# First attention layer of a recommendation kernel as one product per sample, with a four-stage pipeline in source order

## The chip, the cores and the metric

The kernel runs on one core of one Trainium2 chip. The metric is the device time of one execution in microseconds (us). A profile is one execution taken by the hardware profiler; "granted clock" is the share of full TensorE speed that the profile records. Engines in the profile: PE is TensorE, PEld its weight loads, DVE VectorE, ACT ScalarE, POOL GpSimd, SP SyncE.

## The reference

Cut to what matters. B is 16384 samples, F = 69 tokens a sample, E = 96; the first layer has 64 outputs.

```python
u = emb[batch_user]                          # (B, 69, 96), gathered rows
ql = emb[batch_label[:, 0]]                  # (B, 96)
q = broadcast(ql)
z = concatenate([q, u, q - u, q * u])        # 384 wide
h = dice(z @ W1 + b1, a1)                    # first attention layer, 64 wide
att = (h @ W2 + b2) @ W3 + b3
pre = where(batch_user < ITEM_NUM, u * att, 0)
pooled = einsum("gf,bfe->bge", window, pre)  # 10 groups
...                                          # top network: 1056 -> 200 -> 80 -> 1
```

With W1 in four blocks of rows Wq, Wu, Wd, Wp, the first layer before dice is u (Wu - Wd) + (q * u) Wp + q (Wq + Wd) + b1. Below, A is Wu - Wd and Cq is Wq + Wd.

## The kernel before

It works on blocks of 128 samples: 69 tiles of 128 tokens in 18 chunks of up to four tiles, two chunks making a pair, so nine pairs a block. Each tile is fetched by one indirect DMA on GpSimd (a "gather" of 128 rows of 96 floats), transposed by PE, and goes through the hidden layer, the attention weight and the pooling.

```python
def pair_part1(bi, pr, ids, qT):
    u = upool.tile([P, 8, E], F32, tag="u", name=f"u{name}")       # 10 buffers
    ph = ps_h.tile([P, 512], F32, tag="h", name=f"ph{name}")
    for j in range(2):                        # the two chunks: two column halves of PE
        ...
        for i, t in enumerate(ch):
            gather(u[:, 4 * j + i, :], ids[:, bi * NT + t : bi * NT + t + 1])
            nc.tensor.transpose(ptr[:, i * P : (i + 1) * P], u[:, 4 * j + i, :], ident)
        nc.scalar.copy(uT[k][0:E, :], ptr[:, 0:n])
        times_q(quT, uT[k][0:E, :], ch[0] * P, n, qT)      # VectorE: u * q, per sample
        o = ph[j * H1 : (j + 1) * H1, 0:n]
        nc.tensor.matmul(o, caug[bi % 2][:, k, :], uT[k], start=True, stop=False)
        nc.tensor.matmul(o, Wp, quT[:, 0:n], start=False, stop=True)
    ...                                       # dice on ScalarE and VectorE -> y
# pair_part2: attention weights from y (PE), times the masks (VectorE), pooling (PE)
# main loop: part 1 of a pair, then part 2 of the pair before; order left to the framework
```

## Time and profile before

| | before |
|---|---|
| time, median of 3 | 16139.71 us |
| PE busy | 77% |
| POOL busy | 53% |
| VectorE, ScalarE busy | 24%, 19% |
| mean granted clock | 0.598 |
| chain of waits, by engine | PE 60%, unknown release 29% |

The chain is followed back from the last instruction, at each step to what released it; "another core or an unknown queue" in it is a wait whose release the profile doesn't find. The rows of groups read: line, engine, operation, tiles, count, busy us, mean ns of one, then the idle time ahead of them and what ended most of it. The prediction below shows the lines.

Two of its terms, as the trace of the kernel before shows them. "Half clock": the view by windows has a granted clock of 0.50 from 5050 to 5084 us, and 1.00 from 5000 to 5014. "The lock": a gather that starts while VectorE is idle takes 0.946 us in the median; of 466 that start inside L268 (both inputs in SBUF) 255 take over 0.98 us, the longest 1.44; of 347 inside L316 (one input in PSUM) none does.

### The profile page before, as it was taken

Reading aid. Unit: us, or ns where it says so; the run is one execution under the profiler, and the core shown is the slowest. Engines: PE = TensorE matmul, PEld = TensorE weight load, DVE = VectorE, ACT = ScalarE, POOL = GpSimd, SP = SyncE. Lnnn points to the kernel's source line nnn. Section 1 sums busy time; section 2 is a strip of 40 time slices with the busy share of each in tenths; the row PEclk is TensorE's granted clock in tenths of the full one; section 3 lists DMA queues with packets and bytes.
Section 4 is the critical chain, followed back from the end, with each engine's and each line's share of the span. In section 5 each row is a group of like instructions: output and inputs, shape, how many; then the busy total and the mean of one; then the engine's idle time right before and its main releaser. Section 6 shows DMA issues by size and latency. Waiting matters only on the chain.

```text
span 16189.3 us, 144750 instructions
## 1 busy us (share of the span) xinstructions
PE 12511.9 (77%) x56708; PEld 8013.8 (50%) x56708; DVE 3926.3 (24%) x12194; ACT 3123.8 (19%) x5506; POOL 8572.5 (53%) x8973
## 2 busy tenths in 40 slices
PE   6877877778777787777777777778777777787777
PEld 3554544445444554455455454545545545455445
DVE  2222222222222222222222222222222222222222
ACT  1121111111112111211111111112111111121111
POOL 5555555545555555555555555555555545555553
PEclk6566565655656565655555656565555655555656
DMA  1111111111111111111111111111111111111110
GB/s 34 29 29 27 29 29 28 29 26 28 29 28 28 28 29 28 29 29 28 29 28 28 28 28 29 28 29 27 29 29 28 28 27 28 29 29 27 28 29 20
DMA packets 293496, 456.76 MB, mean 28 GB/s; under 512 B 145896, under 2 KB 147151, under 8 KB 292818
## 3 DMA queue, kind: packets, MB, share of 16 engines
q0 software_dynamic: 287008, 440.98, 13.0%
q8 instruction: 453, 7.42, 0.2%
q1 hardware_dynamic: 4144, 5.15, 0.1%
q14 instruction: 225, 1.84, 0.0%
q10 hardware_dynamic: 1666, 1.37, 0.0%
HBM read 446.85 MB, written 0.07 MB: 28 GB/s over the span
## 4 chain that ended last, share of the span: by engine, by line
PE 60%; another core or an unknown queue 29%; issue 4%; DVE 3%; ACT 3%; POOL 1%; DMA 0%; SPq 0%; DVEq 0%; ACTq 0%; POOLq 0%
PE acc L364 14%; PE ph L305 11%; PE ph L304 10%; PE ptr L299 10%; PE patt L327 7%; PE pc L252 3%; PE p L383 3%; ACT g L315 1%; DVE y L316 1%; ACT g L314 1%; DVE pooled L372 1%; PE p L401 1%; ACT uT L300 1%; POOL u L229 1%
## 5 line engine op out<-in xcount | busy, mean ns | idle before, releaser
L229 POOL DMA_INDIRECT u<-in_emb,ids x8832 | 8442.8, 956 | 7443.9 <-PE ptr L299 2421.4
L304 PE MATMUL ph<-uT,caug 105*64 105x512 f32 (+2 forms) x4608 | 3332.6, 894 | 2298.3 <-ACT uT L300 1640.5
L305 PE MATMUL ph<-quT,w 96*64 96x512 f32 (+2 forms) x4608 | 3264.4, 866 | 213.7 <-DVE quT L277 185.3
L364 PEld LDWEIGHTS acc<-rw,u 128*96 128x96 f32 x18176 | 2810.6, 261 | 1142.5 <-issue 522.8
L364 PE MATMUL acc<-rw,u 128*96 128x30 f32 (+2 forms) x18176 | 2853.9, 325 | 391.7 <-DVE rw L345 317.8
L299 PEld LDWEIGHTS ptr<-ident,u 128*96 128x96 f32 x8832 | 1411.3, 185 | 2518.3 <-issue 2070.5
L299 PE MATMUL ptr<-ident,u 128*96 128x128 f32 x8832 | 2290.2, 395 | 178.4 <-issue 106.9
L300 ACT COPY uT<-ptr 96x512 f32<-96x512 f32 (+2 forms) x2304 | 1279.5, 561 | 5911.8 <-PE ptr L299 3795.7
L314 ACT ACTIVATE g<-ph 128x512 f32<-128x512 f32 (+2 forms) x1280 | 719.4, 562 | 6345.9 <-remote 3263.5
L304 PEld LDWEIGHTS ph<-uT,caug 105*64 105x64 f32 x4608 | 573.2, 183 | 2632.9 <-ACT uT L300 1707.8
L327 PEld LDWEIGHTS patt<-v,y 128*128 128x128 f32 x8704 | 1660.0, 284 | 266.4 <-issue 154.5
L327 PE MATMUL patt<-v,y 128*128 128x2 f32 x8704 | 1620.8, 309 | 124.1 <-DVE y L316 116.3
L337 DVE SCALAR_TENSOR_TENSOR w<-patt,bb,mask 128x8 f32<-128x8 f32 (+2 forms) x1280 | 275.2, 223 | 5621.8 <-remote 2807.0
L268 DVE TENSOR_TENSOR quT<-uT,qT 96x414 f32<-96x414 f32 (+3 forms) x2304 | 1363.4, 592 | 2.3
L316 DVE TENSOR_TENSOR y<-ph,g 128x512 f32<-128x512 f32 (+2 forms) x1280 | 822.7, 643 | 1813.7 <-ACT g L315 1549.5
L305 PEld LDWEIGHTS ph<-quT,w 96*64 96x64 f32 x4608 | 641.6, 183 | 822.5 <-issue 444.7
L315 ACT ACTIVATE g<-g,a1c,na1c 128x512 f32<-128x512 f32 (+2 forms) x1280 | 998.9, 780 | 25.2
L277 DVE TENSOR_TENSOR quT<-uT,qT 96x29 f32<-96x29 f32 (+33 forms) x4352 | 747.1, 185 | 801.3 <-ACT uT L300 406.4
L252 PE MATMUL pc<-Cq,qT 96*9 96x64 f32 x4608 | 520.3, 305 | 378.0 <-DVE qT L246 201.5
L372 DVE COPY pooled<-acc 96x430 f32<-96x430 f32 (+1 forms) x384 | 340.0, 886 | 1672.4 <-PE acc L364 1313.9
L383 PE MATMUL p<-pooled,wf 96*100 96x128 f32 x5120 | 727.2, 307 | 22.7 <-DVE quT L277 18.3
L383 PEld LDWEIGHTS p<-pooled,wf 96*100 96x100 f32 x5120 | 700.2, 196 | 34.2 <-DVE quT L277 26.0
(53 smaller groups left out, 2737.7 us busy)
## 6 DMA issues: line engine op xcount, KB each, us to landing
u<-in_emb,ids POOLq DMA_INDIRECT x8832
ids<-in_idx SPq DMA_DIRECT2D x16, 284.0 KB
q<-in_emb,ids POOLq DMA_INDIRECT x135
wf<-in_Wf ACTq DMA_DIRECT2D x1, 825.0 KB
wt<-in_wtok ACTq DMA_DIRECT2D x1, 345.0 KB
uT<-in_rows SPq DMA_DIRECT2D x16, 18.0 KB
out<-res SPq DMA_DIRECT2D x16, 4.0 KB
ts<-in_tsamp ACTq DMA_DIRECT2D x1, 103.5 KB
```

The source lines that it names most:

```text
L229: nc.gpsimd.indirect_dma_start(out=dst, out_offset=None, in_=emb, in_offset=bass.IndirectOffsetOnAxis(ap=index, axis=0),)
L252: nc.tensor.matmul(pc[E : E + NS, k, :], qT[:, s0 : s0 + NS], Cq, start=True, stop=True)
L268: nc.vector.tensor_tensor(dst[:, at : at + m * F].rearrange("e (m f) -> e m f", f=F), src[:, at : at + m * F].rearrange("e (m f) -> e m f" ...
L299: nc.tensor.transpose(ptr[:, i * P : (i + 1) * P], u[:, 4 * j + i, :], ident)
L300: nc.scalar.copy(uT[k][0:E, :], ptr[:, 0:n])
L304: nc.tensor.matmul(o, caug[bi % 2][:, k, :], uT[k], start=True, stop=False)
L305: nc.tensor.matmul(o, Wp, quT[:, 0:n], start=False, stop=True)
L315: nc.scalar.activation(gs, gs, AF.Identity, bias=a1c[lo:hi], scale=na1c[lo:hi])
L316: nc.vector.tensor_mul(y[lo:hi, 0:n], ph[lo:hi, 0:n], gs)
L327: nc.tensor.matmul(patt[:, :, i], y[:, cols], v2, start=True, stop=True)
L364: nc.tensor.matmul(acc[gi][:, (x - a) * G : (z - a) * G], u[:, 4 * j + i, :], rw[:, j, i, (x - lo) * G : (z - lo) * G], start=False, stop= ...
L383: nc.tensor.matmul(p1[:, i, :], wf1[:, k, i * DH : (i + 1) * DH], pooled[:, k, :] if k < G else qT, start=(k == 0), stop=(k == G),)
```

## The change

The intent is to relieve PE. For each sample s a matrix M_s = A + diag(q_s) Wp, with a 97th row q_s Cq + b1, is built by VectorE one block ahead. The hidden layer is then one product per sample instead of two products over all columns of a chunk, and the pieces of the two column halves alternate so that they can run side by side, as two products of different halves do in the trace before (L304 and L305 at 5052.84 us, 1.11 us each). Four stages (fetch, hidden, attend, pool) are one pair apart, and every engine issues in source order.

```diff
-            quT = cpool.tile([E, 512], F32, tag="quT", name=f"quT{name}_{j}")
-            times_q(quT, uT[k][0:E, :], ch[0] * P, n, qT)
-            o = ph[j * H1 : (j + 1) * H1, 0:n]
-            nc.tensor.matmul(o, caug[bi % 2][:, k, :], uT[k], start=True, stop=False)
-            nc.tensor.matmul(o, Wp, quT[:, 0:n], start=False, stop=True)
...
+    def build(qT, M, a, b):
+
+        m = M[0:E, a:b, :]
+        nc.vector.tensor_tensor(
+            m,
+            Wp.to_broadcast([E, b - a, H1]),
+            qT[:, a:b].rearrange("e (m o) -> e m o", o=1).to_broadcast([E, b - a, H1]),
+            ALU.mult,
+        )
+        nc.vector.tensor_tensor(m, m, A.to_broadcast([E, b - a, H1]), ALU.add)
...
+        both = [pieces(2 * pr), pieces(2 * pr + 1)]
+        for n in range(max(map(len, both))):
+            for j in range(2):
+                if n < len(both[j]):
+                    s, a, b = both[j][n]
+                    nc.tensor.matmul(
+                        ph[j * H1 : (j + 1) * H1, a:b],
+                        M[:, s, :],
+                        uT[:, j * 512 + a : j * 512 + b],
+                        start=True,
+                        stop=True,
+                    )
...
+    with tc.manual_schedule():
...
+        for i in range(total + 6):
+            if at := part(i, 3):
...
+                pool(i - 3, pr, us.pop(i - 3), rws.pop(i - 3), accs[n])
+            if at := part(i, 2):
...
+                rws[i - 2] = attend(i - 2, n % NB, pr, round_of(n)[1], ys.pop(i - 2))
+            if at := part(i, 1):
...
+                ys[i - 1] = hidden(i - 1, pr, Ms[n])
...
+            if at := part(i, 0):
+                n, pr = at
+                us[i] = fetch(i, n % NB, pr, round_of(n)[0])
...
+                    if pr in BUILD:
+                        build(qTs[n + 1], Ms[n + 1], *BUILD[pr])
```

The builds come in five bursts a block (pairs 4 to 8) of a multiply and an add over 26 or 25 samples. The 97th row goes through DRAM by SyncE.

## The prediction

> **What bounds the kernel now.** I read the page first (busy shares, chain, groups), then the timeline of some stretches, the rows by form, the waits, and last distances between starts counted over the whole trace. A block is 128 samples; there are 128 blocks, so the span of 16189 us is 126.5 us a block. From the page:
>
> ```profile
> PE 12511.9 (77%) x56708; PEld 8013.8 (50%) x56708; DVE 3926.3 (24%) x12194; ACT 3123.8 (19%) x5506; POOL 8572.5 (53%) x8973
> ...
> PEclk6566565655656565655555656565555655555656
> ...
> PE 60%; another core or an unknown queue 29%; issue 4%; DVE 3%; ACT 3%; POOL 1%; DMA 0%; SPq 0%; DVEq 0%; ACTq 0%; POOLq 0%
> ...
> L229 POOL DMA_INDIRECT u<-in_emb,ids x8832 | 8442.8, 956 | 7443.9 <-PE ptr L299 2421.4
> L304 PE MATMUL ph<-uT,caug 105*64 105x512 f32 (+2 forms) x4608 | 3332.6, 894 | 2298.3 <-ACT uT L300 1640.5
> L305 PE MATMUL ph<-quT,w 96*64 96x512 f32 (+2 forms) x4608 | 3264.4, 866 | 213.7 <-DVE quT L277 185.3
> ```
>
> TensorE carries 60% of the chain at a mean clock of 0.6. Its two largest matmuls, the hidden layer of L304 and L305, are each recorded twice for an f32 product: 2 x 4608 records of 0.87 to 0.89 us. The gathers (L229) sit idle 7444 us, mostly waiting for PE to free `u` (L299, L364). So **PE bounds it, and POOL is the next bound**. The 29% are waits whose release the profile doesn't find. In the row of waits for ACT at L314 they come to 3263 us:
>
> ```profile
> ACT g L314 <- remote: 3263.5, 202, 31.5
> ```
>
> They are late PE semaphores: in the timeline below PE's last hidden matmul before the stall ends near 5057 and the activation that waits for it starts at 5079.
>
> ```profile
> 5050.32 0.63 DVE L268 TENSOR_TENSOR quT<-uT,qT 96x483 f32<-96x483 f32 x1
> ...
> 5050.37 1.40 POOL L229 DMA_INDIRECT u<-in_emb,ids  x1 [0.30 <-issue]
> ...
> 5052.84 1.11 PE L305 MATMUL ph<-quT,w 96*64 96x512 f32 x1
> ...
> 5052.84 1.11 PE L304 MATMUL ph<-uT,caug 105*64 105x512 f32 x1
> ...
> 5055.12 1.97 PE L305 MATMUL ph<-quT,w 96*64 96x512 f32 x2
> ...
> 5060.82 0.94 POOL L229 DMA_INDIRECT u<-in_emb,ids  x1 [0.30 <-issue]
> 5062.07 0.94 POOL L229 DMA_INDIRECT u<-in_emb,ids  x1 [0.30 <-DMA u<-in_emb,ids]
> ...
> 5079.15 0.60 ACT L314 ACTIVATE g<-ph 128x512 f32<-128x512 f32 x1 [25.30 <-remote]
> ```
>
> Three things are to be seen here. Gathers that wait for nothing start 1.25 us apart (0.95 busy, 0.30 issue); over the trace 7801 of 8966 distances are under 1.3 us, mean 1.2508. Two hidden matmuls of different column halves start together and run side by side. And a gather that starts just after a VectorE multiply has begun takes 1.40 us in place of 0.94.
>
> [...] of 7041 gathers that start while VectorE is idle, none takes over 0.98 us; of 347 that start inside L316 (one input in PSUM), none; of 466 inside L268 (both inputs in SBUF) 55%, and with 500 to 600 ns of the multiply still to run the median is 1.37 us. The gather gets through about 0.14 us before the multiply's recorded end. The whole loss before is 95 us. [...] 96-column loads of L364 come 0.160 us apart, 128-column ones of L327 0.213, both at the half clock.
>
> **The change part by part.** Per block:
>
> *Removed on PE*: 36 products of 512 columns or less, 72 records. At the half clock starts are 0.854 to 0.908 apart, so 61 to 65 us (less where halves overlapped); and 72 records of L252, 0.107 us each as 24 in 2.73 us show, 7.7 us:
>
> ```profile
> 4990.79 2.73 PE L252 MATMUL pc<-Cq,qT 96*9 96x64 f32 x24 [9.47 <-DVE qT L246]
> ```
>
> *Added on PE*: one product per sample and chunk. Counting the pieces of the 18 chunks gives 145, mean 60.9 columns, so 290 records, each with a 64-column load. Load: 64/96 x 0.160 = 0.107 us; stream: 61/64 x 0.107 = 0.102. Serial: 290 x 0.107 = 31 us; if the alternating halves overlap in full, 15.5 us.
>
> *Kept on PE at the half clock*: transposes 70 x 0.213 = 14.9; attention 68 x 0.213 = 14.5; pooling 142 x 0.160 = 22.7; top network about 11; the rest 1.6. **PE after: 80 to 96 us a block** at the half clock (before, by the same rule, 132 without overlap, which full-clock stretches cut). [...]
>
> *VectorE*: out go the quT multiplies (1363 + 747 us in L268 and L277, 16.5 us a block). In come ten building instructions in five bursts of a multiply and an add, 26 x 64 = 1664 columns each. From these rows the slope is (651-579)/69 = 1.04 ns a column, the fixed part 148 ns:
>
> ```profile
> L268 DVE TENSOR_TENSOR quT<-uT,qT 96x414 f32<-96x414 f32 x1152 | 667.3, 579 | 0.0
> L268 DVE TENSOR_TENSOR quT<-uT,qT 96x483 f32<-96x483 f32 x896 | 583.7, 651 | 2.3
> ```
>
> So 1.88 us each, 18.5 us a block: VectorE stays near 33 us, not a bound. But both have **both inputs in SBUF** and are three times as long as L268.
>
> *POOL*: 70 gathers a block x 1.2508 = 87.6 us, x 128 = 11207 us (8960 gathers; the 135 split label gathers become 128). This is the floor once PE is under it. To it comes the lock. In a burst the first instruction shuts a gather out until 1.74 us (1.88 - 0.14), the second from 1.80 to 3.54. A gather that wants to start at a random phase f in 0 to 1.25 starts at 1.74, its successor would at 2.99 and starts at 3.54; undisturbed that one had started at f + 1.25. Loss 3.54 - 1.25 - f, mean 1.66 us. 5 bursts x 127 blocks x 1.66 = 1055 us. The 0.4 us multiplies of L345 cost some 30 us more by the same rule.
>
> *The pipeline*: ten `u` tiles let gathers run about seven pairs ahead of the transposes, and four stages in source order give each wait between PE, ACT and VectorE about an iteration (10 us) of slack. The row through DRAM is one small write and read with iterations to spare. ACT is unchanged (24 us a block).
>
> *Sum*: first gather at 26 us + 11207 + 1055 + 30 + some 45 for the last iterations without a gather = 12363 in a profiled run; timed runs are 0.3% shorter (16140 against 16189): 12325. I add 75 us for stretches in which PE holds POOL up: **12400 us**, 23% less.
>
> **Rivals.**
> (a) *The lock costs nothing*, since gathers slip in or the builds fall into POOL's waits: 11.3 ms. For it: only 95 us are lost now. Against: that fits the short multiplies, and if POOL is the bound it has no waits to hide in.
> (b) *PE stays the bound.* For it: the late semaphores come almost only while gathers run (of waits with POOL busy in all the 8 us before, 25% are over 2 us late; with POOL idle 0.1%), and after the change gathers run all the time; pieces have 580 more PE instructions a block than the products that go, less 144 + 144. If the halves don't overlap (96 us) and late semaphores cost the chain its 29% (37 us a block) as now: 96 + 37 = 133 us, 17 ms, no gain. Against: deeper stages hide late releases, and with overlap PE has 80 us against POOL's 96. I give half of the lateness a small chance: 80 + 18 = 98 us, 12.6 ms; 96 + 18 = 114 us, 14.6 ms.
> (c) *VectorE's bursts hold PE up*: 3.7 us before the next attention step's work. They are behind the urgent multiply in source order, and an iteration has 10 us; worth perhaps 0.1 ms.
>
> **Range and chances.** The body lies between rival (a), 11.3, and a mild (b), 13.5, with the lock in the middle; I take 11500 to 13500. Faster than 2% fails only under the full (b): 0.94 faster, 0.04 same, 0.02 slower.
>
> **What would show it.** Right: POOL busy over 75% with next to no gaps for PE; gathers 1.25 us apart outside the builds, and up to 2.7 us long when they start inside one; starts of the hidden pieces in pairs a few ns apart, about 0.05 us a record; the chain on POOL. Wrong: POOL still waiting for PE's L299 or pooling (rival b), or gathers of 0.95 us inside builds (rival a). The prediction falls if PE's late semaphores grow with steady gathers, or if the halves take turns.

## More of the kernel before

The runs of this study met several chips, which the results number. This turned out to matter more than the change itself: the kernel before took 11.47 ms on three of them and 16.1 to 16.4 ms on three others.

## The result, and the profile after

| | before | after |
|---|---|---|
| median | 16130.61 us (4 runs) | 14157.77 us (4 runs) |
| lowest, highest | 16093.38, 16143.22 | 14150.18, 14178.55 |

The ratio is 0.8782, with a 95% interval of 0.8765 to 0.88: 12.2% faster. Ratios here are the mean time of one kernel's fast runs over the mean of the other's fast runs of the same rounds, so not quite the ratio of the medians. The result lies outside the predicted range, 1758 us above the predicted time. Which chip this was is not recorded; by its 16131 us before, it is of the kind called slow below.

From the page of the changed kernel: busy shares, granted clock in 40 slices, chain by engine, and the gathers.

```profile
PE 10058.7 (71%) x80260; PEld 9342.3 (66%) x80260; DVE 4441.9 (31%) x6564; ACT 3142.9 (22%) x5506; POOL 9627.4 (68%) x8966
...
PEclk8555555555555555555555555555555555555555
...
PE 41%; another core or an unknown queue 20%; POOL 17%; issue 12%; DVE 5%; ACT 3%; DMA 2%; SPq 0%; POOLq 0%; ACTq 0%; DVEq 0%
...
L222 POOL DMA_INDIRECT u<-in_emb,ids x8832 | 9480.2, 1073 | 4261.9 <-issue 2428.5
```

PE's busy time has fallen by 2.5 ms, as meant. The mean of a gather has risen from 956 to 1073 ns: 9626.7 us for all 8960, where 0.947 us each would be 8485, so about 1.14 ms of lock, which was predicted. But the gathers still sit idle for 4262 us, of which only 2429 are their own issue; the rest is waiting. The rows of waits (engine, line, what was waited for: us, times, longest) show for what:

```profile
ACT g L304 <- remote: 4204.1, 252, 50.1
...
POOL u L222 <- remote: 862.1, 259, 9.5
...
POOL u L222 <- PE acc L358: 604.5, 137, 11.6
```

"remote" is a release that the profile didn't find. The timeline of one stretch shows what it is (start, duration, engine, line, operation, tiles; at the end the idle time ahead):

```profile
5029.73 2.07 PE L288 MATMUL ph<-uT,M 97*64 97x69 f32 x32
...
5031.73 1.94 PE L274 MATMUL ptr<-ident,u 128*96 128x128 f32 x8
...
5032.74 0.95 POOL L222 DMA_INDIRECT u<-in_emb,ids  x1 [0.30 <-issue]
...
5042.75 0.94 POOL L222 DMA_INDIRECT u<-in_emb,ids  x1 [0.30 <-DMA u<-in_emb,ids]
5043.58 0.60 ACT L304 ACTIVATE g<-ph 128x512 f32<-128x512 f32 x1 [15.46 <-remote]
```

The 32 hidden records take 2.07 us, 0.065 a record where 0.05 was predicted; most start in pairs some 7 ns apart, one pair in 0.107 us, so the halves do run side by side. They end by 5031.80. The activation that waits for exactly these matmuls starts at 5043.58, about 12 us later, and nothing else holds it. Meanwhile the gathers go on 1.25 us apart.

To count this I matched each wait of ScalarE or VectorE on PE's semaphore with the matmul that brings the count, and took its start minus that matmul's recorded end. Call it **lateness**. A prompt wait has 0.04 us. After, 1169 of 2385 such waits are over 1 us late, the worst tenth over 22.9 us; before, 1337 of 4928. (The counts depend on how a wait is matched to its matmul: a second matching, tile by tile, gave 1382 of 2456 and 1141 of 4446.) One episode comes in almost every block (125 in 128), mostly at the first hidden pieces of a block, whose last matmul ends some 6 to 9 us after the last build. In the block above the gathers then run 1.25 us apart for 30 us (5025 to 5055), while the lateness grows from 12 to 25 us, until they have to wait for PE.

A matmul's end in the trace is modelled, so one may ask whether PE itself is slow or only its completion reaches the others late. The trace also records each update of PE's semaphore. In this profile 3420 of the 12142 recorded updates come within 40 ns of the one before, though no two of the matmuls that make them end within 100 ns of each other. In a profile without lateness (the changed kernel on chip 12, below) none of 13100 updates comes within 100 ns of the one before, and all but two follow a matmul's recorded end by 10 to 20 ns. The updates of ScalarE and VectorE are prompt in both profiles, 99% of them within 13 ns. (Updates that are missing from a trace, 8% here, can only widen the gaps.) So PE's completions are held back and let through in bunches, closer together than PE was ever seen to make them: at least there, it is the completion that is late. Where it is held isn't visible.

### The profile page after: what moved, and what is told of

The parts are those of the page before. It is cut to its first block, busy times and chain, and to the rows that moved or that the text cites.

```text
span 14156.7 us, 187662 instructions
## 1 busy us (share of the span) xinstructions
PE 10058.7 (71%) x80260; PEld 9342.3 (66%) x80260; DVE 4441.9 (31%) x6564; ACT 3142.9 (22%) x5506; POOL 9627.4 (68%) x8966
## 3 DMA queue, kind: packets, MB, share of 16 engines
q14 instruction: 192, 1.57, 0.0%
## 4 chain that ended last, share of the span: by engine, by line
PE 41%; another core or an unknown queue 20%; POOL 17%; issue 12%; DVE 5%; ACT 3%; DMA 2%; SPq 0%; POOLq 0%; ACTq 0%; DVEq 0%
POOL u L222 17%; PE acc L358 10%; PE ph L288 9%; PE patt L316 8%; PE ptr L274 7%; PE p L377 4%; DMA u<-in_emb,ids 1%; DVE M L263 1%; DVE M L257 1%; DVE y L306 1%; ACT g L305 1%; ACT uT L276 1%; PE p L397 1%; ACT g L304 1%
## 5 line engine op out<-in xcount | busy, mean ns | idle before, releaser
L222 POOL DMA_INDIRECT u<-in_emb,ids x8832 | 9480.2, 1073 | 4261.9 <-issue 2428.5
L316 PE MATMUL patt<-v,y 128*128 128x2 f32 x8704 | 1814.7, 327 | 2543.8 <-DVE y L306 1985.8
L288 PE MATMUL ph<-uT,M 97*64 97x69 f32 (+7 forms) x37120 | 2540.4, 304 | 897.9 <-issue 639.5
L288 PEld LDWEIGHTS ph<-uT,M 97*64 97x64 f32 x37120 | 2302.0, 213 | 1038.9 <-issue 736.5
L304 ACT ACTIVATE g<-ph 128x512 f32<-128x512 f32 (+2 forms) x1280 | 722.1, 564 | 9052.7 <-remote 4204.1
L274 PE MATMUL ptr<-ident,u 128*96 128x128 f32 x8832 | 2075.7, 399 | 220.6 <-issue 162.2
L263 DVE TENSOR_TENSOR M<-M,A 96x1664 f32<-96x1664 f32 (+1 forms) x640 | 1190.8, 1861 | 22.1
L257 DVE TENSOR_TENSOR M<-w,qT 96x1664 f32<-96x1664 f32 (+1 forms) x640 | 1184.0, 1850 | 0.0
L305 ACT ACTIVATE g<-g,a1c,na1c 128x512 f32<-128x512 f32 (+2 forms) x1280 | 999.2, 781 | 43.1
L377 PE MATMUL p<-pooled,wf 96*100 96x128 f32 x5120 | 930.9, 359 | 14.2 <-issue 12.7
L377 PEld LDWEIGHTS p<-pooled,wf 96*100 96x100 f32 x5120 | 881.9, 238 | 22.4 <-issue 17.9
L334 DVE TENSOR_TENSOR rw<-R,w 128x240 f32<-128x240 f32 (+2 forms) x1280 | 481.2, 376 | 43.8
```

Source lines behind the costliest of these rows:

```text
L222: nc.gpsimd.indirect_dma_start(out=dst, out_offset=None, in_=emb, in_offset=bass.IndirectOffsetOnAxis(ap=index, axis=0),)
L257: nc.vector.tensor_tensor(m, Wp.to_broadcast([E, b - a, H1]), qT[:, a:b].rearrange("e (m o) -> e m o", o=1).to_broadcast([E, b - a, H1]), ...
L263: nc.vector.tensor_tensor(m, m, A.to_broadcast([E, b - a, H1]), ALU.add)
L274: nc.tensor.transpose(ptr[:, k * P : (k + 1) * P], u[:, 4 * j + k, :], ident)
L288: nc.tensor.matmul(ph[j * H1 : (j + 1) * H1, a:b], M[:, s, :], uT[:, j * 512 + a : j * 512 + b], start=True, stop=True,)
L304: nc.scalar.activation(gs, ph[lo:hi, 0:n], AF.Sigmoid, scale=S_DICE)
```

## The experiments

The theories at the start: **A**, undisturbed gathers make PE's completions late; **B**, the slow stretches are PE's own, set off by its order of work, such as a new block's first products. Kernels without real gathers or builds give a wrong result. The comparison with the reference still accepted some of them, so "correct" says little about those.

### Without gathers, with plain loads, without builds, halves apart

Four edits of the changed kernel:

```diff
 e1_no_gather: ten fixed u tiles, gathered for the first ten pairs only
+                if i < 10:
                 gather(u[:, 4 * j + k, :], ids[:, ...])
 e2_plain_load: r is the first of 128 consecutive rows, another 128 for each tile
-                gather(u[:, 4 * j + k, :], ids[:, ...])
+                nc.sync.dma_start(out=u[:, 4 * j + k, :], in_=emb[r : r + P, :])
 e3_no_build:
-                        Ms[n + 1] = head_row(n + 1, qTs[n + 1])
-                    if pr in BUILD: ...
+                        Ms[n + 1] = Ms[0]
 e4_halves_apart:
-        for n in range(max(map(len, both))):
-            for j in range(2):
+        for j in range(2):
+            for n in range(len(both[j])):
```

> The changed kernel without its gathers: ten fixed u tiles, gathered once for the first ten pairs and then read again and again (wrong result on purpose, everything else kept). Theory A (the late PE semaphores come from undisturbed runs of gathers): no wait on PE is more than about 2 us late, and the kernel runs at PE's own pace, 80 to 96 us a block by my sum, so 10.3 to 12.3 ms. Theory B (the slow stretches are PE's own, set off by the first products of a new block or the like): they stay, one a block of about 22 us, so 80 + 22 = 102 us a block, about 13 ms or more.

> Each gather replaced by a plain load of 128 consecutive rows (same bytes, same u tile, issued by SyncE; wrong result on purpose). GpSimd does nothing, but the rows still arrive. Theory A1 (GpSimd's work for a gather slows PE): as without gathers, 10.3 to 12.3 ms, no late waits. Theory A2 (rows arriving in SBUF slow PE): slow stretches stay, 13 to 14.2 ms. Theory B: slow stretches stay too, 13 ms or more; the run without gathers tells A2 from B.

> The per-sample matrices and their row are made once and used for all blocks (wrong result on purpose): no builds, so no lock on the gathers. If the lock loss of 1142 us lies on the path in full: 14158 - 1142 = 13.0 ms. Theory A (undisturbed gathers make PE late): gathers run at 1.25 us everywhere, slow stretches come more often, and most of the gain is lost: 13.6 to 14.2 ms. Theory B (a new block's first products): nothing depends on the gathers, 13.0 ms, and if the first use of a freshly built matrix is what sets it off, no slow stretches and 11.4 ms.

> The hidden pieces of one column half all before those of the other, so no two neighbours run side by side. My sum has 31 us a block instead of 15.5 for the hidden pieces: if PE is on the path all the time, 15.5 us x 128 = 2.0 ms longer, 16.1 ms; if PE is on it for about half (chain PE 41% plus late semaphores 20%), 0.8 to 1.2 ms longer; if GpSimd is the bound and PE has room, 14.2 ms.

| run, chip 11 | median us | ratio to before |
|---|---|---|
| kernel before | **11475.79** | |
| no gathers | 9053.01 | 0.7889 |
| plain loads | 9454.46 | 0.8245 |
| no builds | 11288.4 | 0.9837 |
| halves apart | 12442.29 | 1.0841 |

The surprise is the first row: **the same kernel before took 11476 us here, not 16131**. In none of the four traces is a wait on PE over 1 us late. So this chip could not decide between A and B, and it asked a new question: is the lateness a matter of the chip? It did measure other terms. Without gathers PE alone sets the end; its share of the page and the chain are:

```profile
PE 8978.2 (99%) x80260; PEld 8621.2 (95%) x80260; DVE 4465.7 (49%) x6574; ACT 3108.8 (34%) x5506; POOL 214.7 (2%) x211
...
PE 98%; POOL 1%; issue 0%; DMA 0%; DVE 0%; ACT 0%; POOLq 0%
```

That is 71 us a block at a mean clock of 0.628, below the predicted 80 to 96. No builds gives 11288, beside the predicted floor of 11207 + 30 + 26 + 45 = 11308.

### The changed kernel again, builds with PSUM operands, and the framework's own order

```diff
 f2_psum_build: label and A are copied to PSUM (the small PSUM tiles share one bank)
-            qT[:, a:b].rearrange("e (m o) -> e m o", o=1)...
+            kk[:, n % 2, a:b].rearrange("e (m o) -> e m o", o=1)...
-        nc.vector.tensor_tensor(m, m, A.to_broadcast([E, b - a, H1]), ALU.add)
+        nc.vector.tensor_tensor(m, m, Ak.to_broadcast([E, b - a, H1]), ALU.add)
 f3_tile_order:
-    with tc.manual_schedule():
+    if True:
```

> The changed kernel itself, unaltered, because in the first four experiments the kernel before took 11476 us where the blind measurement had 16131, and no wait on PE was late. Theory P (late PE semaphores belong to the place the kernel runs at, not to the kernel): if the kernel before is again near 11476, this one has no late waits and is bound by GpSimd with the lock: 11288 (no builds) + about 1140 (lock) = 12.43 ms, 8% SLOWER than before; if before is near 16131, this one is at 14.16. Theory Q (the change takes PE off the bound everywhere): under 11.47 ms in either.

> The builds read the label and the constant A from PSUM, so that neither of the two instructions has both inputs in SBUF; the small PSUM tiles share one bank. Theory L (two SBUF inputs lock the gathers out): gathers stay at 0.95 us inside builds, the lock loss of about 1140 us vanishes; with no late PE semaphores 11.3 to 11.4 ms; with them between 13.0 and 14.2. Rival (any long VectorE instruction delays a gather, or the loss is elsewhere): as the changed kernel.

> The new first layer, but every engine's order left to the framework's own scheduling instead of source order. If the four-stage source order is what hides waits, PE stalls come in and this is slower than the changed kernel by 3% or more; if GpSimd with the lock is the bound anyway, it is within 1%.

| run, chip 12 | median us | ratio to before |
|---|---|---|
| kernel before | 11468.32 | |
| changed kernel | **12432.06** | 1.0841 (1.0823 to 1.0859) |
| builds with PSUM operands | **11290.35** | 0.9842 (0.9826 to 0.9859) |
| framework's own order | 12771.51 | 1.1134 |

Theory P came true: on such a chip the change makes the kernel **8.4% slower**, at 12432 us, within 0.3% of the 12400 that were predicted for the other. Chain and gathers of the changed kernel here, from its page, then a stretch with two builds from its timeline:

```profile
POOL 55%; issue 21%; DMA 13%; PE 11%; DVE 0%; POOLq 0%; ACT 0%; ACTq 0%; DVEq 0%
...
L222 POOL DMA_INDIRECT u<-in_emb,ids x8832 | 9527.9, 1079 | 2691.6 <-issue 2501.4
```

```profile
5019.14 1.87 DVE L257 TENSOR_TENSOR M<-w,qT 96x1664 f32<-96x1664 f32 x1
5019.24 2.58 POOL L222 DMA_INDIRECT u<-in_emb,ids  x1 [0.30 <-issue]
...
5021.04 1.89 DVE L263 TENSOR_TENSOR M<-M,A 96x1664 f32<-96x1664 f32 x1
5022.13 1.61 POOL L222 DMA_INDIRECT u<-in_emb,ids  x1 [0.30 <-issue]
```

POOL now has no idle time but its issue (2691.6, of which 2501 are issue), and the chain is on it. The gather at 5019.24 starts 0.10 us after the multiply, and takes 2.58 us instead of 0.95; the next runs into the add. With the PSUM operands the builds are as long, and the gathers pass straight through (1890 of them start inside a build, and none takes over 0.96 us; of 1247 in the changed kernel, all but one take over 0.98):

```profile
L232 POOL DMA_INDIRECT u<-in_emb,ids x8832 | 8386.3, 950 | 2691.5 <-issue 2469.7
```

```profile
5001.11 1.86 DVE L268 TENSOR_TENSOR M<-w,kk 96x1664 f32<-96x1664 f32 x1
...
5001.65 0.95 POOL L232 DMA_INDIRECT u<-in_emb,ids  x1 [0.30 <-issue]
...
5003.01 1.88 DVE L274 TENSOR_TENSOR M<-M,kk 96x1664 f32<-96x1664 f32 x1
```

The gathers of the two runs differ by 9648.8 - 8507.2 = 1141.6 us, and the two times by 1141.7 us. So **the lock costs 1.14 ms, is due to the two SBUF inputs, and lies wholly on the path** on this chip. The rival that any long VectorE instruction holds up a gather is refuted. Against the kernel before, the PSUM version is 1.6% faster.

The framework's own order is 2.7% slower, between the two cases I had expected. Of the 339 us, 307 are again longer gathers (9956.0 against 9648.8 us): I take it that its builds fall worse for the gathers, but didn't follow it up.

### A slow chip, first meeting

> The kernel before, unaltered, for its profile at a place where it takes about 11.47 ms. If its late semaphores are what held it at 16.1 ms, then without them GpSimd bounds it already: chain on POOL, gathers 1.25 us apart nearly everywhere, 8967 x 1.2508 = 11216 us, plus about 26 us start, 45 us drain and 95 us lock = 11.38 ms, near 11.47. If instead PE still bounds it, the chain is on PE and gathers have waits for PE of over 1 ms. If it runs where it takes 16.1 ms, its profile repeats the first one.

> The version with label and A in PSUM once more, in case this chip is one where the kernel before takes 16.1 ms. There: if late PE semaphores come from undisturbed gathers, lateness takes the lock's place and the time stays at 13.6 to 14.2 ms; if they are tied to a block's start, 14158 - 1142 = 13.0 ms. Where before takes 11.47 ms: 11.29 ms again.

> No gathers after the first ten pairs (as in the first experiment, wrong result on purpose), and the hidden pieces of one column half all before those of the other. With PE alone on the path this measures the overlap of the two halves by itself: 9053 us with halves alternating; my sum gives 15.5 us x 128 = 2.0 ms more at the half clock, less if the clock is higher (x 0.5/0.63 = 1.6 ms): 10.6 to 11.0 ms. If neighbours on different halves gain nothing, 9.05 ms. If before takes 16.1 ms here: any wait on PE over 2 us late without gathers would show that gathers are not needed for lateness.

The edit of the third is that of halves apart, on top of no gathers. Chip 8 was of the slow kind: the kernel before took 16351.84 us in the median of 7 runs (16337.85 with its profile, with 1396 of 4928 waits over 1 us late). The PSUM version, unaltered, took **14228.92** instead of 11290.35, ratio 0.8709 (0.868 to 0.8738). The lock is gone, and the time is about that of the changed kernel with the lock: lateness has taken the lock's place, as theory A had it; 2053 of 2612 waits are over 1 us late. The largest row of its waits:

```profile
ACT g L315 <- remote: 4882.5, 510, 22.4
```

Without gathers, with the halves apart, the four runs took 9069.74 to 9956.66 us, and 4 of 1958 waits were over 1 us late, all in the first 137 us, where the gathers of the first ten pairs still run. Those runs fell in different states (clocks 0.674 to 0.751), so I draw nothing from their time, except that on this slow chip, too, PE is prompt once the gathers have stopped.

### Ten kinds of work in one run

To compare everything on one chip, one kernel has stretches of 12 blocks, all with the fixed u tiles and the PSUM builds, except where named:

```diff
+    psum: gather       lock: gather, builds as in the change    none: no gather
+    load: nc.sync.dma_start of 128 rows     half: every other gather
+    slow: nc.gpsimd.memset(scr[:, 0:256], 0.0), then the gather
+    thin: gather of 8 of the 96 columns     memset: 8 x nc.gpsimd.memset(u, 0.5) a pair
+    none_apart, psum_apart: as none and psum, hidden halves one after the other
```

> One run with ten kinds of stretches of 12 blocks each (wrong result on purpose), to have all of them on one chip: (psum) gathers and builds with a PSUM operand; (lock) gathers and the change's builds; (none) no gathers; (load) plain loads by SyncE in place of the gathers; (half) every other gather; (slow) a GpSimd memset before each gather; (thin) gathers of 8 of the 96 columns; (memset) no gathers, eight GpSimd memsets of u per pair; (none_apart) and (psum_apart) as none and psum, hidden halves one after the other; last 8 blocks as psum. Where before takes 11.47 ms: psum 88 us a block, lock 97, none and load 71 to 74, half 71 to 80, none_apart 12 to 16 above none, and no late waits anywhere. Where before takes over 16 ms, theory A1 (GpSimd's work for a gather makes PE late): load without late waits, near none; thin as late as psum (about 110 us a block), half in between. Theory A2 (rows arriving in SBUF): load as late as psum, thin not late. Theory A3 (any steady GpSimd work): memset late too.

> The ten kinds of stretches again, in an order that leaves real rows in u for all but the last (psum, lock, none, load, half, none_apart, slow, psum_apart, thin, memset), because in the first such run the stretch none_apart read constants that a memset had left and had a granted clock of 0.74. If that clock came from the constants: none_apart at a clock near 0.59 and 10 us a block above none; if it came from the halves not running side by side: 0.74 again and no longer than none. Where before takes over 16 ms: theory A1 (GpSimd's work for a gather makes PE late): load near none without late waits, thin late like psum; A2 (arriving rows): load late, thin not; A3 (any steady GpSimd work): memset late too; slow tells whether gathers 1.6 us apart leave PE in time.

> The ten kinds of stretches as in the run before, for a slow place. There theory A1 (GpSimd's work for a gather makes PE late): load near none (75 us a block) without late waits, thin late like psum (about 110); A2 (arriving rows): load late, thin not; A3 (any steady GpSimd work): memset late too; slow tells whether gathers 1.6 us apart leave PE in time (102 us a block) or not (110 or more). At another place: the same as the last run, within 1 us a block.

The first two met chips 3 and 11 (before: 11476.61 and 11476.58 us), the third chip 7 (before: 16131.81). The second and third run the same kernel. Time of a block is from the starts of y's multiplies, over nine blocks of each stretch; each run is one execution, and the stretches that chips 3 and 11 share agree within 0.4 us a block, but for the two with halves apart:

| stretch | chip 11, us a block | chip 7, us a block | chip 7: waits over 1 us late |
|---|---|---|---|
| psum | 87.79 | **111.71** | 81 of 126 |
| lock | 96.49 | 114.20 | 63 of 143 |
| none | 75.09 | **74.00** | 0 of 156 |
| load | 76.21 | 75.01 | 0 of 157 |
| half | 75.11 | 79.00 | 28 of 153 |
| none_apart | 74.85 | 71.66 | 0 of 144 |
| slow | 102.11 | 106.08 | 115 of 150 |
| psum_apart | 87.48 | 113.94 | 80 of 139 |
| thin | 87.61 | 112.22 | 82 of 128 |
| memset | 75.11 | 74.22 | 0 of 154 |

On chip 11 (and chip 3) no wait is late in any stretch. On chip 7 the stretches, in the view by windows (from and to, length, then busy us and count of PE, PE loads, VectorE, ScalarE and POOL; granted clock, DMA share, GB/s): psum, none, load, thin, memset.

```profile
339.20:1344.60 1005.40, 725.88 (x5643) 678.70 (x5643) 313.59 (x470) 215.27 (x388) 598.08 (x631) 0.57 0.15 33
...
2928.40:3594.40 666.00, 657.94 (x5645) 627.77 (x5644) 315.46 (x470) 218.59 (x388) 8.52 (x9) 0.60 0.01 3
3820.80:4495.80 675.00, 661.71 (x5645) 628.72 (x5644) 315.47 (x469) 218.46 (x388) 8.52 (x9) 0.60 0.22 49
...
9279.60:10289.60 1010.00, 715.65 (x5643) 668.09 (x5643) 313.50 (x470) 215.44 (x388) 598.58 (x631) 0.58 0.07 5
10514.20:11182.20 668.00, 660.44 (x5645) 630.65 (x5644) 316.32 (x470) 218.51 (x388) 485.86 (x657) 0.60 0.02 4
```

The plain loads bring 49 GB/s, more than the gathers' 33, and PE is prompt. The thin gathers bring 5 GB/s, and PE is as late as ever. GpSimd memsets, with POOL busy 73% of the time, do nothing. A count that needs no matching agrees: of the updates of PE's semaphore, 936 of 1372 come within 100 ns of the one before in psum, 967 of 1379 in thin, 489 of 1301 in lock, and none in none, load and memset. So on the slow chips it is **the gather as such, however many bytes it brings**, that makes PE late: A1 stands; A2 (arriving rows), A3 (any GpSimd work, as far as memsets tell) and B (PE's own order) fall. Thin and load differ in the engine that issues them, GpSimd and SyncE. Which part of a gather does the harm is not shown: thin names 128 rows as psum does, and no run issued a plain DMA from GpSimd or a gather of fewer rows. The granted clock doesn't show the lateness: 0.57 and 0.60 on chip 7, 0.56 and 0.59 on chip 11.

A second finding is in none and none_apart. On chip 11, from the same view:

```profile
2392.50:3068.30 675.80, 668.32 (x5645) 637.68 (x5644) 315.79 (x470) 218.57 (x388) 8.49 (x9) 0.59 0.01 3
...
5105.30:5778.90 673.60, 666.67 (x5645) 637.74 (x5644) 312.88 (x470) 217.99 (x388) 8.81 (x10) 0.69 0.01 4
```

PE is busy 99% of both and does the same work, in 75.09 and 74.85 us a block. With the halves side by side the granted clock is 0.59, one after the other 0.69. So **running the halves side by side gains no time** here: the granted clock is lower with it. (An estimate from these numbers: 75.09 x 0.59 = 44 us of full clock against 74.85 x 0.69 = 52, so the overlap itself is real.) On chip 7 side by side was even the slower, 74.00 against 71.66 us. In the first mixed run none_apart came after a stretch that left constants in u, and had 71.65 us at 0.74; since the second run, with real rows, had 0.69, and chip 7, also with real rows, 0.74, the clock comes mainly from the order. Not from it alone: the run without gathers above had the same order on the same chip 11, and 0.628 and 71 us a block; why is open. The halves-apart kernel above, at 12442 against 12432 us on two fast chips, says nothing on this, since POOL bounds both (43% and 55% of their chains, the most of any engine).

### How much gathering PE stands

> Stretches of 12 blocks with PSUM builds: all gathers (psum), 6, 4 and 2 of each 8 (s6, s4, s2), all gathers with a GpSimd memset of 128, 256, 384, 512 columns before each (d128 to d512), eight memsets at once before each pair (pause8), and none (wrong result on purpose). Where before takes over 16 ms: if each gather costs PE a fixed time, us a block falls in a line from 112 to 74: s6 102, s4 93, s2 84, and spacing gathers out doesn't help; if only long undisturbed runs of gathers make PE late, s6 and s4 fall well below the line (the last run had 79 for 4 of 8), and d384, d512 and pause8 have no late waits and are as long as GpSimd's own work. Elsewhere: psum 88, s6 to none 75, d128 to d512 96 to 125, no late waits.

```diff
+    s6, s4, s2: 6, 4, 2 of each 8 gathers     none: no gather
+    d128 ... d512: nc.gpsimd.memset(scr[:, 0:128 ... 512], 0.0) before each gather
+    pause8: 8 memsets of 256 columns before each pair's gathers
```

Chip 10 was slow (before: 16394.71 us).

| stretch | gathers a block | us a block | waits over 1 us late |
|---|---|---|---|
| psum | 70 | 113.65 | 82 of 130 |
| s6 | 54 | 93.58 | 71 of 131 |
| s4 | 36 | 79.26 | 28 of 157 |
| s2 | 19 | 75.49 | 1 of 160 |
| none | 1 | 75.09 | 0 of 153 |
| d128 | 70 | 110.97 | 90 of 144 |
| d256 | 70 | 110.63 | 126 of 174 |
| d384 | 70 | **109.49** | **0 of 227** |
| d512 | 70 | 116.67 | 0 of 236 |
| pause8 | 70 | 115.48 | 95 of 150 |

A fixed cost per gather is refuted: s6, s4 and s2 lie at 94, 79 and 75 where a line would have 105, 95 and 85 (113.65 and 75.09 as its ends). It is the rate: at 109.49 / 70 = 1.56 us from gather to gather all waits are prompt, and POOL sets the pace; with the shorter memset, whose own pace is 1.46 us (102.11 / 70 on chip 11), 126 of 174 waits are over 1 us late. Eight gathers together and then a pause don't help, though their own pace averages about the same (an estimate: 8 x 1.25 us and eight memsets of 0.33 us, as measured on chip 3, make 1.58 us a gather). With all 70 gathers a block takes 109 to 117 us on this chip whatever is done, that is 1.56 to 1.67 us for each gather.

### The kernel before on a fast chip

> The kernel before with a profile once more; the last time it met a slow place. Where it takes 11.47 ms: GpSimd bounds it, chain mostly on POOL, gathers 1.25 us apart, no wait on PE over 1 us late; the rival is PE at a high granted clock (0.69 in the result lists, where the slow place had 0.60) with POOL waiting on it. Where it takes over 16 ms: as the first profile.

> The kernel before with a profile, for a place where it takes 11.47 ms (the last two tries met slow places). There: GpSimd bounds it, chain mostly POOL, issue and DMA as in the changed kernel's profile at 12.43 ms, gathers 1.25 us apart nearly everywhere; the rival is PE with POOL waiting on it for over 1 ms.

> The kernel before with a profile, for a place where it takes 11.47 ms. There: GpSimd bounds it, chain mostly POOL, issue and DMA, gathers 1.25 us apart nearly everywhere and 8967 x 1.2508 = 11.22 ms of them, no wait on PE over 1 us late; the rival is PE with POOL waiting on it for over 1 ms.

> The kernel before with a profile, last try for a place where it takes 11.47 ms. There: GpSimd bounds it, chain mostly POOL, issue and DMA, gathers 1.25 us apart nearly everywhere and 8967 x 1.2508 = 11.22 ms of them, no wait on PE over 1 us late; the rival is PE with POOL waiting on it for over 1 ms.

I wanted one profile of the kernel before where it takes 11.47 ms. All four met slow chips (7, 10, 10, 7), with 16192.4, 16305.73, 16297.61 and 16086.49 us and profiles like the first one. What bounds it on a fast chip is left as an estimate from the trace before: 8967 gathers x 1.2508 = 11216 us, with 26 + 45 + 95 of start, drain and lock 11.38 ms, which is 0.8% under the measured 11.47. That leaves PE next to nothing to add, by this estimate.

Medians of the kernel before, by chip (without the five extra profiled runs, 16086 to 16338 us, all on slow chips):

| chip | kernel before, us |
|---|---|
| 3, 11, 12 | 11477, 11476 and 11477, 11468 |
| 7, 8, 10 | 16132 and 16136, 16352, 16395 |
| the two measurements (chip not recorded) | 16140, 16131 |

Nothing in between was seen, and chips 7 and 11, met twice, gave the same both times.

## Why the prediction was wrong, step by step

- **The bound before, "PE bounds it, and POOL is the next bound".** True of the trace that I had, but a good part of it was lateness. On fast chips the same kernel runs at 11.47 ms, next to POOL's floor, which is 29% less. The unknown releases in the chain before were 29% too, which fits, but no run tests it. The prediction had read them rightly as late PE semaphores that come while gathers run, but not as something that another chip might not have.
- **PE after, 80 to 96 us a block.** PE alone takes 71 to 75. The term for the halves (31 us, or 15.5 if they overlap) was wrong in kind: side by side or apart, the block took 75.09 and 74.85 us, as the clock moved from 0.59 to 0.69. This didn't matter for the sum.
- **The builds, 1.88 us each.** Measured 1.85 and 1.86.
- **Two slips without effect on the sum.** The products of L252 are 36 records a block (4608 in 128 blocks), not 72, so 3.9 us and not 7.7 were removed; and 3 of the 7041 gathers with VectorE idle did take over 0.98 us.
- **POOL's floor, 11207 us plus ends.** Right: 11288 without builds and 11290 without the lock, against 11308 summed.
- **The lock, 1055 us for the builds.** Right in kind, 8% too small: 1141.6. (The 30 us for the short multiplies of L345 are in both runs of that difference.)
- **The sum, 12363, and 12400 with PE's share.** Right on a fast chip, 12432. Wrong on the chip of the result, 14158.
- **The step that failed is the last term of the sum: "I add 75 us for stretches in which PE holds POOL up".** On the slow chip this term was not 75 us but about 1.8 ms: before their starts the gathers sit idle for 4262 us there and for 2692 us on chip 12, 1.57 ms more, and PE's lateness is what they wait for. Rival (b) was right about the late semaphores, though not about halves that take turns, and its reason against was the error: "deeper stages hide late releases". They don't, because the lateness isn't a fixed delay that a stage of slack can absorb. It sets in when gathers follow each other at less than some 1.46 to 1.56 us (d256 and d384 on chip 10: 126 of 174 waits late, and 0 of 227), and, as in the block shown above, grows until the gathers have to wait. So the better the gathers are freed, the later PE gets: on chip 7, 81 of 126 waits were late in psum and 63 of 143 in lock. The prediction's own 37 us of lateness a block, added to PE alone at 74.00, makes 111, and psum on chip 7 took 111.71. That is luck: 37 us was 29% of the block before, and after the change the unknown releases are 20% of the chain, 22 us a block.
- **The sequel: the lock is almost free on a slow chip.** On chip 7, psum and lock differ by 2.5 us a block, little more than psum and psum_apart do there (2.2); on chip 11 they differ by 8.7. This is why the lock, the main term of the prediction, showed in the gathers' durations after the change but hardly set the time.
- **The direction.** "Faster" held on the slow kind of chip and is the reverse on the fast kind, where the change costs 8.4%. The prediction had a chance of 0.02 for that, since it took the base of 16.1 ms as the kernel's own.

What stays open: what in a gather holds PE's completions back on chips 7, 8 and 10 and not on 3, 11 and 12, where they are held, and whether PE itself ever stalls besides. I tried to model the lateness in the trace after the change as a backlog that each gather adds to and that drains steadily. The best fit (1.4 us a gather) had a correlation of 0.59 with the measured lateness, too little to call it shown.

The version with PSUM operands beats the kernel before on both kinds, 11290 against 11468 and 14229 against 16352. It beats the changed kernel by 9.2% on the fast kind; on the slow kind the two are close (111.71 against 114.20 us a block within one run, and 14229 and 14158 us on different chips).

## What to carry to other kernels

Before a base time is explained, measure it on more than one chip: a release that the profile can't find, next to steady indirect DMAs, went here with the chip, and made the same kernel take 40% longer (16.13 ms on chip 7, 11.48 on chip 11). When VectorE works beside GpSimd gathers, try one of its two inputs in PSUM; on chip 12 that took 1.14 ms off with one small copy a block. A count of TensorE time at a fixed clock is only half a count: work laid side by side had a granted clock of 0.59, one after the other 0.69, and nothing was gained (75.09 and 74.85 us a block, chip 11).
